# K and V of all four groups of the first batch made plainly, and another written order

## The chip, the cores and the metric

The kernel runs on one core of one Trainium2 chip. The metric is the device time of one execution in microseconds; the median of several executions is compared. The core has five engines with instruction streams of their own: TensorE (PE in the profile, with its weight loads as PEld), VectorE (DVE), ScalarE (ACT), GpSimd (POOL) and SyncE (SP), which here only issues transfers.

## The reference

A cross-attention block with four batches, 512 queries, 512 keys and a width of 512 (16 heads of 32), all in fp32:

```python
x = layer_norm(hidden, ln1_w, ln1_b)
q, k, v = x @ q_w + q_b, enc @ k_w + k_b, enc @ v_w + v_b      # split into 16 heads of 32
attn = softmax(where(mask, q @ k.T / sqrt(32), -max))
hidden = (attn @ v) @ cproj_w + cproj_b + hidden
y = layer_norm(hidden, ln2_w, ln2_b)
return hidden + gelu(y @ fc_w + fc_b) @ proj_w + proj_b        # inner width 2048
```

## The kernel before

The 16 heads are taken in four groups of four, and a batch's four groups give 16 steps called w (w = 4 x batch + group). For each w the kernel makes K, V and q (a product of the group's 128 weight columns with the transposed encoder or input tile), then four score steps, one per row tile of 128 queries. What is called "0:3" below is row tile 3 of w = 0. A score step is four products of 32 rows, one per head (L581). A softmax tile per head follows: DVE adds the mask and finds the minimum (L589), ACT takes the exponential (L592). The tiles are then transposed in blocks of 32 on DVE (L600, L607; L610 for the row sums), POOL copies the blocks that stay on their partitions (L617), twelve transfers of SP exchange the others, and PE multiplies with V (the attend, L639); DVE scales by the sums (L645). Behind the four groups come the output projection (L445), LN2 (statistics L343 and L344 on DVE, deviation L351 and L359 on POOL, normalisation L364 on DVE, turns L371 on PE), and two layers of the MLP (L694).

K and V come in two ways. Plainly, by `prep_k` (four products of 512 columns, L481, evicted by ACT at L484) and `prep_v` (sixteen products of 128 columns, L492, evicted at L498), one group at a time. Or for a pair p of groups (p = w // 2) by `kv`: a scheme of Strassen's kind with seven products of half-size blocks instead of eight (L524). It needs sums of the encoder tile's blocks (`e_sums`) and of the two groups' weight blocks (`kv_sums`), all on POOL (L332, L335), and joins of the results (`k_join`, `v_join`), three parts copied from PSUM and two additions on DVE, of 128x512 and of 128x256 (L332). In the first batch, groups 0 and 1 are made plainly and groups 2 and 3 as a pair; in the later batches all are pairs.

What stands when on each engine is written out by hand as one long string of tokens, `ORDER`. Each token is a name with its indices and names a generator; meeting it runs the generator to its next yield, which records the instructions of one step. Engines run their own instructions in the order in which they were recorded:

```python
    for token in ORDER.split():
        if token not in begun:
            name, *rest = token.split(":")
            begun[token] = takes[name](*map(int, rest))
        if begun[token] is not None:
            next(begun[token], None)
```

The tokens that matter here: `pk:w` and `pv:w` (plain K and V), `k:p`, `v:p` (pairs), `ks:p`, `vs:p`, `es:b` (sums), `kj:p`, `vj:p` (joins), `wk:w`, `wq:w`, `wv:w` (weight loads), `q:w`, `u:w:t` (score step), `x:w:t` (its softmax tiles, one head at a time), `r` (transposes), `d`, `e`, `a` (stay, exchange, attend), `s2:b`, `r2:b`, `n2:b`, `t2:b` (LN2), `lh:b` (the residual rows of x), `f:b:c` (MLP).

Buffers set waits too. The weights of step w lie in one of two buffers per kind, by w % 2, so a load for w = 2 has to wait until the product of w = 0 is done. Rows of x share a ring of six. PSUM has four banks for scores and a ring of four for everything else.

Of the kernel before, what the change touches and what calls it, by code (L numbers as in the profile page):

```python
# [20 lines left out]
P = 128  # L21
# [39 lines left out]
pk:0 s1:0 s1:0 s1:0 s1:0 r1:0 n1:0 wk:2 pk:0 n1:0 n1:0 n1:0 pv:0 pk:1 pk:1 t1:0:1 t1:0:1 t1:0:0 t1:0:3 t1:0:0 t1:0:2  # L61
  m:0 qb t1:0:2 pv:0 t1:0:3 q:0 q:0 k:1
u:0:0 x:0:0 x:0:0 x:0:0 x:0:0 wk:3 wv:1 lx:2 wq:1 lx:1 pv:1 wv:2 wq:2 lf:0:1 lx:1 wv:3 lc r:0:0 r:0:0
u:0:1 q:1 x:0:1 x:0:1 x:0:1 x:0:1 r:0:1 r:0:1 q:1
u:0:2 ks:1 vb:0 ks:1 r:0:1 v:1 vj:1 r:0:1 pv:1 x:0:2 x:0:2 x:0:2 es:0 m:0 vs:1 es:0 ks:1 es:0 k:1 es:0 vs:1 x:0:2 vs:1
  vs:1 ks:1 d:0:0 d:0:0
u:0:3 s1:1 x:0:3 kj:1 v:1 k:1 x:0:3 kj:1 r:0:2 v:1 k:1 vj:1 r:0:2 x:0:3 x:0:3 r:0:3 v:1
u:1:0 kj:1 vj:1 kj:1 k:1 r:0:3 r:0:3 vj:1 v:1 vj:1 lx:1 wq:3 q:3 s1:1 r:0:3 x:1:0 x:1:0 q:3 x:1:0 x:1:0
u:1:1 e:0:0 e:0:0 le:1 e:0:0 lx:1 s1:1 s1:1 r:1:0 wk:4 lh:0 x:1:1 x:1:1 x:1:1 kj:1 x:1:1 kj:1 r:1:1 r:1:0 d:0:1 q:2
  d:0:1 le:1 es:1 vb:0 le:1 lf:0:3 wk:5 le:1 r1:1 es:1 es:1 es:1  # L70
u:1:2 ts:1 ts:1 e:0:1 e:0:1 x:1:2 r:1:1 r:1:1 x:1:2 r:1:1 e:0:1 ks:2 ts:1 ks:2 ks:2 k:2 a:0:0 q:2 x:1:2 x:1:2 a:0:0
  d:1:0
u:1:3 kj:2 x:1:3 x:1:3 k:2 k:2 kj:2 vj:1 r:1:2 x:1:3 x:1:3 r:1:3 r:1:2
u:2:0 x:2:0 r:1:3 wv:4 lt:1 lt:1 lt:1 e:1:0 lb:1 lb:1 a:0:1 k:2 kj:2 v:2 x:2:0 a:0:1 d:1:0 ks:2 na:1 x:2:0 x:2:0
u:2:1 r:1:3 x:2:1 kj:2 e:1:0 e:1:0 na:1 k:2 a:1:0 wa:1 x:2:1 r:1:3 r:2:0 kj:2 x:2:1 x:2:1 wa:1 na:1 r:2:0
u:2:2 x:2:2 wa:1 wq:4 lt:1 na:1 r:2:1 r:2:1 a:1:0 wa:1 x:2:2 x:2:2 d:1:1 q:4 x:2:2 r:2:1 r:2:1 kj:2
u:2:3 x:2:3 vj:2 x:2:3 wq:5 e:1:1 e:1:1 e:1:1 wk:7 wk:6 wv:5 d:1:1 d:2:0 r:2:2 x:2:3 x:2:3 vs:2 ks:3 vs:2 vs:2 ks:3
  vb:1 e:2:0 e:2:0 q:5 e:2:0 wq:7 d:2:0 vs:2 r:2:3 q:4 r:2:3 r:2:2 a:1:1
u:3:0 x:3:0 v:2 v:2 vj:2 a:1:1 x:3:0 r:2:3 x:3:0 x:3:0
u:3:1 x:3:1 x:3:1 r:2:3 r:3:0 a:2:0 v:2 vj:2 x:3:1 x:3:1 a:2:0  # L80
u:3:2 k:3 r:3:0 r:3:1 x:3:2 x:3:2 vj:2 v:2 q:5 r:3:1 x:3:2 kj:3 x:3:2
u:3:3 r:3:1 vj:2 r:3:1 vj:2 x:3:3 d:2:1 vb:1 ks:3 d:2:1 lf:0:0 wq:6 e:2:1 lh:0 e:2:1 e:2:1 e:3:0 e:3:0 e:3:0 wv:6
  x:3:3 d:3:0 d:3:0 s1:2 r:3:2 x:3:3 x:3:3 r:3:2 q:6 a:2:1
u:4:0 m:1 r:3:3 a:2:1 r:3:3 r:3:3 q:7 k:3 x:4:0 x:4:0 q:6 r:3:3 x:4:0 x:4:0
u:4:1 lx:2 r:4:0 wv:7 lt:2 vs:3 ks:3 a:3:0 k:3 x:4:1 q:7 x:4:1 x:4:1 x:4:1
u:4:2 r:4:0 r:4:1 a:3:0 x:4:2 c:0:1 kj:3 k:3 x:4:2 x:4:2 r:4:1 x:4:2 kj:3
u:4:3 lt:2 d:3:1 d:3:1 cb:0 cb:0 r:4:1 vs:3 vs:3 vs:3 r:4:1 d:4:0 vb:2 s1:2 x:4:3 d:4:0 c:0:1 c:0:0 e:3:1 e:3:1 e:3:1
  r:4:2 x:4:3 kj:3 v:3 k:3 lx:2 lf:0:1 lf:0:0 lf:0:3 lh:0 lh:0 cb:0 cb:0 e:4:0 e:4:0 lx:2 e:4:0 lf:0:2 fs:0:0 c:0:0
  r:4:3 kj:3 s2:0 x:4:3 x:4:3 s1:2 a:3:1 vj:3 v:3 v:3 a:3:1 kj:3 r:4:2 r:4:3 vj:3
u:5:0 v:3 r:4:3 s2:0 s1:2 c:0:2 x:5:0 x:5:0 vj:3 r:4:3 vb:2 fs:0:0 r1:2 x:5:0 wv:8 x:5:0 vj:3 r:5:0  # L90
u:5:1 v:3 x:5:1 vj:3 x:5:1 r:5:0 c:0:2 x:5:1 x:5:1 r:5:1 c:0:3 c:0:3 d:4:1 d:4:1 wk:8 le:2 le:2 wk:9 e:4:1 le:2 le:2
  c:0:0 c:0:1 es:2
u:5:2 a:4:0 ts:2 ts:2 k:4 kj:4 r:5:1 x:5:2 s2:0 x:5:2 x:5:2 s2:0 x:5:2 r:5:1 r:5:1 a:4:0 ks:4 es:2 ks:4 es:2 ks:4 ks:4
  es:2 c:0:3 k:4 r2:0 c:0:2 e:4:1 k:4
u:5:3 kj:4 k:4 kj:4 e:4:1 r:5:2 e:5:0 e:5:0 e:5:0 r:5:2 x:5:3 x:5:3 kj:4 vj:3 x:5:3 a:4:1 x:5:3
u:6:0 n2:0 x:6:0 n2:0 k:4 kj:4 n2:0 n2:0 t2:0:3 t2:0:0 t2:0:3 t2:0:0 t2:0:1 t2:0:2 r:5:3 x:6:0 x:6:0 x:6:0 r:5:3
# [924 lines left out]
```

## Time and profile before

| | |
|---|---|
| median of 3 runs | 764.81 us (762.33 to 766.98) |
| profiled execution | 765.29 us |
| its span | 763.5 us, mean granted clock 0.998 |
| ACT, POOL busy | 411.4 us, 431.5 us |
| DMA | 162.19 MB, mean 212 GB/s |

Busy times are of one profiled execution, from its first instruction to its last. A matmul's end is modelled, so a busy PE can still be a waiting one. Every fp32 matmul has two records, so a count of x8 in the chain of waits stands for four products. Line numbers are those of the kernel before.

### The profile page before, as it was taken

What the parts mean: (1) busy time and instruction counts of PE and PEld (TensorE: products, weight loads), DVE (VectorE), ACT (ScalarE), POOL (GpSimd) and SP (SyncE); (2) the same over time, 40 slices, a digit from 0 to 9 for tenths busy, and PEclk for the clock granted to TensorE, in tenths of its full rate; (3) what the DMA queues carried; (4) which work ended last, traced back from release to release, by engine and by line L of the source; (5) the groups of instructions that cost most, each with busy time, mean ns of one, the idle gap of its engine ahead of it and who ended that gap; (6) DMA issues with size and microseconds to landing.
All of it is one profiled execution on the core that took longest, in us unless ns stands there. A gap on an engine that the chain in (4) does not pass through costs nothing.

```text
span 763.5 us, 14364 instructions
## 1 busy us (share of the span) xinstructions
PE 750.3 (98%) x4953; PEld 548.2 (72%) x4953; DVE 614.5 (80%) x1238; ACT 411.4 (54%) x981; POOL 431.5 (57%) x473
## 2 busy tenths in 40 slices
PE   9999999989999999999999999999999999999998
PEld 6565444646576656776565776767889999999997
DVE  3799999999889889987969787736688789888773
ACT  2567666455998776868867788732234321111111
POOL 1678866876978496889576566894201122131331
PEclk9999999999999999999999999999999999999999
DMA  6788979886777978695785778799535666688565
GB/s 227 236 242 225 236 201 252 232 230 184 242 200 194 281 204 247 196 281 154 214 245 171 218 256 261 215 254 353 167 131 165 214 209 123 213 184 257 140 123 121
DMA packets 72134, 162.19 MB, mean 212 GB/s; under 512 B 11960, under 2 KB 24656, under 8 KB 70400
## 3 DMA queue, kind: packets, MB, share of 16 engines
q1 hardware_dynamic: 56864, 131.44, 58.5%
q0 software_dynamic: 15056, 29.84, 16.0%
q8 instruction: 39, 0.64, 0.3%
q14 instruction: 31, 0.25, 0.1%
q10 hardware_dynamic: 144, 0.02, 0.0%
HBM read 73.95 MB, written 25.18 MB: 130 GB/s over the span
## 4 chain that ended last, share of the span: by engine, by line
PE 87%; DMA 4%; DVE 3%; ACT 3%; SPq 1%; issue 1%; POOL 0%; DVEq 0%; POOLq 0%; ACTq 0%
PE acc L694 36%; PE sc L694 12%; PE acc L524 9%; PE sc L581 8%; PE acc L445 7%; PE acc L639 6%; PE acc L573 5%; DMA ext<-encT_dram 2%; SPq L329 1%; ACT ptt L592 1%; PE acc L371 1%; DVE ptt L589 1%; PE acc L481 1%; PE acc L492 1%; DMA gd<-st 1%
## 5 line engine op out<-in xcount | busy, mean ns | idle before, releaser
L592 ACT ACTIVATE ptt<-ptt,mn 128x512 f32<-128x512 f32 x256 | 182.9, 716 | 52.8 <-DVE mn L589 52.2
L589 DVE CUSTOM_DVE_ANT_0 ptt<-sc,mix 128x512 f32<-128x512 f32 x256 | 165.4, 678 | 21.3 <-PE sc L581 18.6
L617 POOL COPY swap<-swap 32x1088 f32<-32x1088 f32 x128 | 140.2, 1095 | 36.1 <-DVE swap L610 29.6
L720 ACT COPY st<-acc 128x256 f32<-128x256 f32 x128 | 46.1, 367 | 96.3 <-PE acc L694 85.7
L720 ACT COPY xn<-acc 128x128 f32<-128x128 f32 x100 | 24.1, 267 | 133.0 <-PE acc L694 129.3
L600 DVE STREAM_TRANSPOSE swap<-ptt 128x1024 f32<-128x1024 f32 x64 | 79.0, 1235 | 5.2 <-ACT st L746 1.2
L581 PE MATMUL sc<-pbt 32*128 32x512 f32 x512 | 82.0, 647 | 0.0
L607 DVE STREAM_TRANSPOSE swap<-ptt 128x1024 f32<-128x1024 f32 x64 | 78.3, 1223 | 0.6 <-ACT ptt L592 0.6
L748 POOL DMA_DIRECT2D gd<-st x32 | 23.7, 743 | 86.5 <-ACT st L746 65.7
L694 PE MATMUL acc<-ys,ws 128*128 128x256 f32 x256 | 63.4, 383 | 0.5 <-ACT st L720 0.5
L639 PE MATMUL acc<-swap,mix 128*32 128x256 f32 x1024 | 61.9, 382 | 0.9 <-DMA ext<-x_t_dram 0.6
L573 PE MATMUL acc<-ext,ptt 128*128 128x512 f32 x128 | 58.8, 600 | 1.4 <-DVE mn L589 0.8
L445 PE MATMUL acc<-mix 128*128 128x512 f32 x128 | 58.3, 601 | 0.0
L694 PE MATMUL acc<-yT,pbt 128*128 128x256 f32 x240 | 58.1, 383 | 0.0
L694 PEld LDWEIGHTS acc<-ys,ws 128*128 128x128 f32 x256 | 47.4, 190 | 13.1 <-ACT st L720 4.7
L639 PEld LDWEIGHTS acc<-swap,mix 128*32 128x32 f32 x1024 | 30.4, 109 | 33.5 <-issue 9.7
L694 PEld LDWEIGHTS acc<-yT,pbt 128*128 128x128 f32 x240 | 44.5, 190 | 13.7 <-issue 5.1
L906 POOL DMA_DIRECT2D swap<-xn x18 | 22.4, 1434 | 52.8 <-DVE xn L332 18.7
L592 ACT ACTIVATION_READ_ACCUMULATOR ptt<-ptt,mn 128x1 f32 x256 | 48.3, 189 | 0.0
L906 POOL DMA_DIRECT2D yT<-xn x15 | 18.3, 1547 | 48.5 <-DVE yT L332 17.9
L573 PEld LDWEIGHTS acc<-ext,ptt 128*128 128x128 f32 x128 | 23.3, 190 | 30.9 <-issue 23.3
L445 PEld LDWEIGHTS acc<-mix 128*128 128x128 f32 x128 | 23.2, 190 | 31.0 <-issue 28.6
(163 smaller groups left out, 1601.9 us busy)
## 6 DMA issues: line engine op xcount, KB each, us to landing
swap<-swap SPq DMA_DIRECT2D x384, 136.0 KB, 3.3
gd<-st POOLq DMA_DIRECT2D x32, 512.0 KB, 3.9
swap<-gd SPq DMA_DIRECT2D x12, 1024.0 KB, 6.9
pbt<-fc_w_dram SPq DMA_DIRECT2D x40, 256.0 KB, 4.6
xn<-x_dram SPq DMA_DIRECT2D x32, 256.0 KB, 3.9
ext<-fc_w_dram SPq DMA_DIRECT2D x24, 256.0 KB, 3.7
swap<-xn POOLq DMA_DIRECT2D x18, 256.0 KB, 4.7
ptt<-k_w_dram SPq DMA_DIRECT2D x16, 256.0 KB, 5.2
```

The lines of the kernel that those rows point to most:

```text
L445: nc.tensor.matmul(acc, oT[:, g, ts(t, P)], wc[:, g, :], start=(g == 0), stop=(g == NG - 1))
L524: nc.tensor.matmul(out_, i, j, start=(k + t == 0 and not more), stop=(k == 1), skip_group_check=more or t > 0)
L573: nc.tensor.matmul(acc, S["wq", w][:, d, :], xT[:, d, :], start=(d == 0), stop=(d == ND - 1))
L581: nc.tensor.matmul(sc[h], S["qT", w][r, ts(qt, P)], S["kT", w][r, :], start=True, stop=True)
L589: nc.vector.tensor_tensor_reduce(out=s, in0=sc[h], in1=mb, scale=1.0, scalar=FMAX, op0=ALU.add, op1=ALU.min, accum_out=mn)
L592: nc.scalar.activation(s, s, AF.Exp, bias=mn, scale=-1.0, accum_out=S["sums", w][:, qt, h : h + 1])
L600: nc.vector.transpose(*two_heads[0])
L607: nc.vector.transpose(*two_heads[1])
L617: nc.gpsimd.tensor_copy(pT[ts(i, HD), i], tb[ts(i, HD), i])
L639: nc.tensor.matmul(av[ts(h, HD), : 2 * P].rearrange(shape, **kw), v[:, t, ts(h, HD)], p[t][h], start=(t == 0), stop=(t == NT - 1),)
L694: nc.tensor.matmul(o, x[:, k], w, start=(k == 0 and not more), stop=(k == n - 1), skip_group_check=more)
L720: nc.scalar.copy(g[:, i], S["qa", *key])
```

## The change

Only the string `ORDER` differs. The tokens of the pair p = 1 and of the first batch's encoder sums are gone, and plain ones stand in their place; the string as a whole (2569 tokens before, 2543 now) is written anew in another sequence, in all batches. The number of tokens of every kind that differs:

| tokens | before | now |
|---|---|---|
| `k:1`, `v:1` | 5, 5 | 0, 0 |
| `kj:1`, `vj:1` | 6, 6 | 0, 0 |
| `ks:1`, `vs:1`, `es:0` | 4, 4, 4 | 0, 0, 0 |
| `pk:2`, `pk:3`, `pv:2`, `pv:3` | 0 | 2 each |

```diff
-u:0:1 q:1 x:0:1 x:0:1 x:0:1 x:0:1 r:0:1 r:0:1 q:1
-u:0:2 ks:1 vb:0 ks:1 r:0:1 v:1 vj:1 r:0:1 pv:1 x:0:2 x:0:2 x:0:2 es:0 m:0 vs:1 es:0 ks:1 es:0 k:1 es:0 vs:1 x:0:2 vs:1
...
+u:0:1 x:0:1 x:0:1 x:0:1 x:0:1 r:0:1 q:1
+u:0:2 pk:2 pk:3 r:0:1 q:1 r:0:1 r:0:1 x:0:2 x:0:2 x:0:2 x:0:2
...
```

In the rows below, line numbers of the kernel now are two higher than those of the kernel before (L481 is L483 now, L492 is L494, L524 is L526, L573 is L575, L581 is L583, and L343, L344, L364, L589 are L345, L346, L366, L591). `sc` are the score banks, `acc` the ring of four, `ext` the encoder and input tiles, `ptt` weights and softmax tiles, `pbt` K and q.

**TensorE, from q of group 0 (the first row) on.** Before:

```order
L573 MATMUL acc_79<-ext,ptt 128x512 x4
L524 MATMUL acc_78<-ext,ptt 128x256 x2
L581 MATMUL sc_74<-pbt 128x512
L581 MATMUL sc_75<-pbt 128x512
L581 MATMUL sc_76<-pbt 128x512
L581 MATMUL sc_77<-pbt 128x512
L492 MATMUL acc_80<-ptt,ext 128x128 x16
```

Now:

```order
L575 MATMUL acc_78<-ext,ptt 128x512 x4
L494 MATMUL acc_80<-ptt,ext 128x128 x16
L583 MATMUL sc_74<-pbt 128x512
L583 MATMUL sc_75<-pbt 128x512
L583 MATMUL sc_76<-pbt 128x512
L583 MATMUL sc_77<-pbt 128x512
L494 MATMUL acc_81<-ptt,ext 128x128 x16
L483 MATMUL acc_79<-ext,ptt 128x512 x4
```

Ahead of the first score step the pair's first product (two of 256 columns) is replaced by the whole plain V of group 2, and behind it the plain K of group 2 has come to V of group 1.

**TensorE, the third and fourth score step (0:2 and 0:3) and the product ahead of each.** Before:

```order
L573 MATMUL acc_81<-ext,ptt 128x512 x4
L581 MATMUL sc_74<-pbt 128x512
L581 MATMUL sc_75<-pbt 128x512
L581 MATMUL sc_76<-pbt 128x512
L581 MATMUL sc_77<-pbt 128x512
L524 MATMUL acc_79<-ptt,ext 128x128 x4
L524 MATMUL acc_81<-ext,ptt 128x256 x4
L581 MATMUL sc_74<-pbt 128x512
```

Now:

```order
L575 MATMUL acc_78<-ext,ptt 128x512 x4
L583 MATMUL sc_74<-pbt 128x512
L583 MATMUL sc_75<-pbt 128x512
L583 MATMUL sc_76<-pbt 128x512
L583 MATMUL sc_77<-pbt 128x512
L483 MATMUL acc_81<-ext,ptt 128x512 x4
L583 MATMUL sc_74<-pbt 128x512
```

Between the two steps stood the first products of the V and K pair; now the plain K of group 3 stands there. The first row in both is q of group 1.

**DVE, between the last LN2 statistics of the first batch (BN_AGGR) and the first LN2 normalisation (TENSOR_SCALAR).** Before, the end of that piece; its twelve rows are preceded by six more that lead back to the BN_AGGR (one softmax tile, and the rows L607, L610, L645, L600):

```order
L607 STREAM_TRANSPOSE swap<-ptt 128x2x4x4x32
L589 ISA ptt,mn_3_0_1441<-sc_74,mix 128x512
L589 ISA mn_3_0_1441 128x1
L589 ISA ptt,mn_3_1_1444<-sc_75,mix 128x512
L589 ISA mn_3_1_1444 128x1
L332 TENSOR_TENSOR pbt<-acc_78,pbt 128x2x256
L332 TENSOR_TENSOR mix<-acc_79,mix 128x256
L589 ISA ptt,mn_3_2_1449<-sc_76,mix 128x512
L589 ISA mn_3_2_1449 128x1
L589 ISA ptt,mn_3_3_1468<-sc_77,mix 128x512
L589 ISA mn_3_3_1468 128x1
L364 TENSOR_SCALAR xn_85<-xn_85,mv_0_1200,rs_0_1406 128x512
```

Now, the whole piece:

```order
L345 BN_STATS st_0_3_1392<-xn_85 128x6
L346 BN_AGGR mv_0_1235<-st_0_3_1392 128x2
L612 STREAM_TRANSPOSE swap<-mix 128x2x4x32
L602 STREAM_TRANSPOSE swap<-ptt 128x2x4x4x32
L591 ISA ptt,mn_3_0_1408<-sc_74,mix 128x512
L591 ISA mn_3_0_1408 128x1
L591 ISA ptt,mn_3_1_1411<-sc_75,mix 128x512
L591 ISA mn_3_1_1411 128x1
L366 TENSOR_SCALAR xn_82<-xn_82,mv_0_1235,rs_0_1402 128x512
```

The statistics and the normalisation have come closer together: one small and one large transpose and two softmax tiles (an L591 pair each) are left between them. The normalisation also stands ahead of the last two softmax tiles of step 5:3, where it stood behind them.

On SP, the loads of V weights for groups 2 and 1 now come first behind the mask, and a load of `lh:0` stands ahead of the K weights of group 2.

More of the change, by code (lines that the diff above doesn't have):

```diff
@@ L68 @@
[L68 to L96, printed above, removed]
@@ new lines @@
+u:8:0 k:5 kj:5 f:0:4 a:6:1 j:0:4 g:0:2 g:0:4 r:7:2 x:8:0 x:8:0 x:8:0 r:7:3 x:8:0 a:6:1 r:7:3
+u:8:1 kj:5 lx:3 wv:10 e:7:0 wv:11 e:7:0 wq:10 e:7:0 v:5 x:8:1 e:7:1 e:7:1 e:7:1 lf:1:0 lf:0:6 lf:0:5 d:7:0 vs:5 cb:1
+  vs:5 vb:4 g:0:2 vs:5 vb:3 fs:0:3 fs:0:3 fs:0:3 d:7:1 fs:0:3 cb:1 d:7:1 cb:1 f:0:3 r:8:0 x:8:1 x:8:1 x:8:1 j:0:4
+  a:7:0
+u:8:2 g:0:4 r:8:0 r:8:1 a:7:0 s1:3 x:8:2 x:8:2 j:0:3 c:1:0 c:1:0 v:5 f:0:3 f:0:3 vj:5 j:0:3 r:8:1 x:8:2 x:8:2 r:8:1
+  s2:1 r:8:2
+u:8:3 f:0:3 j:0:3 r:8:1 vs:5 v:5 d:8:0 d:8:0 g:0:4 j:0:3 f:0:3 j:0:3 x:8:3 a:7:1 x:8:3 vj:5 x:8:3 x:8:3 r:8:2 r:8:3
+  j:0:3
@@ new lines @@
+u:12:1 j:1:2 d:11:0 vs:7 vs:7 vs:7 d:11:1 d:11:1 f:1:2 q:13 j:1:2 g:1:2 r:12:0 r:12:0 x:12:1 q:13 x:12:1 j:1:2 x:12:1
+  vj:7 v:7 x:12:1
+u:12:2 r:12:1 r:12:1 x:12:2 x:12:2 x:12:2 v:7 a:11:0 a:11:1 vj:7 x:12:2
+u:12:3 lf:2:4 g:1:2 v:7 vj:7 r:12:2 a:11:0 r:12:1 r:12:1 x:12:3 lf:1:5 e:12:0 vj:7 c:2:0 cb:2 g:1:2 fs:1:3 d:12:0
+  x:12:3 x:12:3 x:12:3 a:11:1 c:2:0 fs:1:3 fs:1:3 fs:1:3
+u:13:0 f:1:3 v:7 g:1:1 vj:7 g:1:1 r:12:3 r:12:3 j:1:3 r:12:2 x:13:0 f:1:3 f:1:3 c:2:2 j:1:3 r:12:3 vj:7 x:13:0 r:12:3
+  x:13:0 x:13:0
```

280 lines of the change are left out of this document (148 added, 132 removed).

## The prediction

> **What bounds the kernel now.** I read the page's busy shares first, then the busy times of four stretches, then what the vector engine waits for in the second of them, then the chain of waits.
>
> ```profile
> PE 750.3 (98%) x4953; PEld 548.2 (72%) x4953; DVE 614.5 (80%) x1238; ACT 411.4 (54%) x981; POOL 431.5 (57%) x473
> ```
>
> (The stretches are cut at the start of the first softmax tile, of the fourth step's first tile, and where TensorE resumes behind the first LN2; columns are PE, PEld, DVE, ACT, POOL busy, granted clock, DMA share, GB/s.)
>
> ```profile
> 24.30:37.80 13.50, 13.50 (x80) 8.54 (x80) 13.37 (x32) 9.71 (x26) 6.86 (x9) 1.00 0.74 218
> 37.80:173.10 135.30, 129.15 (x834) 71.48 (x833) 130.18 (x286) 83.63 (x223) 105.00 (x110) 1.00 0.85 229
> 173.10:500.00 326.90, 325.07 (x2043) 214.52 (x2044) 274.05 (x580) 254.38 (x556) 240.12 (x270) 0.99 0.77 223
> 500.00:763.50 263.50, 259.67 (x1897) 238.43 (x1895) 189.78 (x325) 58.42 (x171) 73.00 (x74) 1.00 0.68 189
> ```
>
> TensorE (PE) reads 98% busy, but its weight loads (PEld) fill only 71.48 of 135.30 us in the second stretch, against 238.43 of 263.50 at the end. VectorE (DVE) fills 130.18 of those 135.30. So from 37.8 to 173.1 us two engines could be the limit, and the waits say which:
>
> ```profile
> DVE pbt L332 <- ACT pbt L722: 1.0, 2, 0.8
> DVE ptt L589 <- PE sc L581: 0.8, 4, 0.3
> DVE swap L600 <- DMA ext<-x_t_dram: 0.8, 1, 0.8
> ```
>
> (waiter, released by: us in total, times, longest.) These are the three largest; DVE waits for nothing longer than 0.8 us and for TensorE 0.8 us in all. It is DVE that runs through here. The chain, in order of time (start, us, what), shows how it is entered and left:
>
> ```profile
> 9.89 3.57 PE acc L492 x32
> 13.46 3.44 PE acc L481 x8
> 18.90 3.44 PE acc L573 x8
> 22.34 0.86 PE acc L524 x4
> 23.21 1.07 PE sc L581 x8
> 24.28 3.77 PE acc L492 x32
> 29.12 3.63 PE acc L573 x8
> 36.63 1.43 PE sc L581 x8
> 53.76 0.60 DVE ptt L589
> 55.93 1.15 DVE swap L600
> 57.08 1.14 DVE swap L607
> 169.66 3.42 DVE xn L364 x3
> 178.12 1.86 PE acc L639 x32
> ```
>
> The entry: up to the fourth score step (group 0, row tile 3, at 36.63) every piece is TensorE. Then the chain goes over softmax pieces (L589) and transposes (L600, L607). The exit: the LN2 normalisation of the first batch (L364, three in 3.42 us) ends at 173.1, TensorE's turns (L371) wait for it, and behind them TensorE keeps going to the end. So the time is a sum of three: TensorE up to the fourth score step, DVE from there to the LN2 normalisation, TensorE from its turns to the end. The change moves all three.
>
> **Term 1, TensorE in front: +6.4 us.** After the same start (q of group 0 ends at 22.34 in both orders) the old order has two light products (0.86) ahead of the first scores, and its fourth score step starts 14.29 later. The new order puts the plain V of group 2 (sixteen 128-column products as in the L492 row, 3.57), a score step (1.07), V of group 1 (3.57), K of group 2 (four 512-column products, L481, 3.44), a score step, q of group 1 (L573, 3.44), a score step and K of group 3 (3.44) ahead of it: 3.57+1.07+3.57+3.44+1.07+3.44+1.07+3.44 = 20.67. That is 6.38 more. The old rows for V and q there read 3.77 and 3.63, 0.2 over their clean value; with that on all five big products it is 7.4, my upper end. Is DVE really late by all of it? Its first softmax tile moves by 3.57-0.86 = 2.7, from 24.3 to 27.0; up to the fourth step's scores it had 13.37 us of work in the old order (first row of the stretches) and has one transpose (1.15) more in the new one, so it is through at 41.5. The scores come at 22.34+20.67 = 43.0 and about 1.1 later reach DVE, as in the old order (36.63 to 37.8). So it stands for some 2.5 us, and TensorE sets the term. If the scores were ready sooner, DVE's own work would still make it 2.7+1.15 = 3.9, the lower end.
>
> The load of group 2's V weights can add to this. It reuses group 0's buffer, so the queue sends it only when V of group 0 is done, about 13.5; it must be there at 22.34.
>
> ```profile
> ptt<-v_w_dram SPq DMA_DIRECT2D x16, 256.0 KB, 4.2
> ```
>
> Such a load lands 4.2 us after its issue (median), so 4.6 us are to spare and I take nothing. The residual load of x that now goes ahead of the K weights of group 2 waits for the first turns (done at 18.90); those weights are wanted only at 30.6, eleven microseconds on.
>
> **Term 2, DVE: -7.1 us.**
>
> ```profile
> L332 DVE TENSOR_TENSOR pbt<-acc,pbt 128x512 f32<-128x512 f32 x7 | 4.8, 690 | 2.5 <-ACT pbt L722 2.5
> L332 DVE TENSOR_TENSOR mix<-acc,mix 128x512 f32<-128x512 f32 x7 | 4.8, 682 | 4.7 <-ACT mix L720 4.6
> L332 DVE TENSOR_TENSOR mix<-acc,mix 128x256 f32<-128x256 f32 x7 | 2.8, 407 | 3.5 <-PE acc L524 3.5
> L332 DVE TENSOR_TENSOR pbt<-acc,pbt 128x256 f32<-128x256 f32 x7 | 2.8, 404 | 0.0
> L343 DVE BATCH_NORM_STATS2 st<-xn 128x6 f32<-128x512 f32 x32 | 21.6, 674 | 9.0 <-DMA xn<-x_dram 9.0
> L344 DVE BATCH_NORM_AGGREGATE mv<-st 128x2 f32<-128x6 f32 x32 | 5.8, 182 | 1.1
> ```
>
> Removed: the joins of one K pair and one V pair, 0.690+0.404+0.682+0.407 = 2.18. Moved out of the stretch, counted from the two orders: one statistics pair to the front (0.674+0.182 = 0.86), one transpose to the front and one behind (1.15+1.14 = 2.29), and three softmax tiles (3 x 0.60 = 1.80) behind the LN2 normalisation, which now stands earlier among them. Sum 7.13. What was moved is not won: the front pieces lie in term 1, those behind are no longer on the path because TensorE is the fuller engine there. The uncertain part is the waits: the three rows above make 2.6 us. The new order could lose them all or have as much again, so the ends are -9.7 and -4.5.
>
> **Term 3, TensorE behind: +2.9 us.** From the LN2 turns on the new order has one more score step (1.07) and one more attend (L639, 1.86); all other products are the same in number. Their order is rewritten in all later batches too. TensorE was busy there for 325.07 of 326.90 and 259.67 of 263.50 us, so a better order has little to win; I take nothing for it.
>
> The TensorE work added is in terms 1 and 3 already. On its own it is small: two K products pairwise plain are 2 x 3.44 = 6.88 against fourteen 256-column products, and V 2 x 3.57 = 7.14 against twenty-eight 128-column ones at 3.57/16 = 0.223, which is 6.25.
>
> ```profile
> 218.73 2.59 PE acc L694 x12
> ```
>
> Six 256-column products take 2.59, so fourteen take 6.04, and the whole adds 0.84+0.89 = 1.73 us.
>
> **At nothing:** GpSimd (POOL) loses the four sums of the encoder tile and the eight of the weights.
>
> ```profile
> L332 POOL TENSOR_TENSOR ws<-ptt 128x256 f32<-128x256 f32 x14 | 10.4, 743 | 25.1 <-DMA ptt<-v_w_dram 15.6 <-DMA ptt<-k_w_dram 6.0 <-PE acc L524 3.3
> L335 POOL TENSOR_TENSOR mix<-ext,mix 128x512 f32<-128x512 f32 x8 | 10.3, 1286 | 5.5 <-DMA ext<-encT_dram 5.5
> ```
>
> About 8 x 0.74 + 4 x 1.28 = 11 us. It is busy 105.00 of 135.30 and none of DVE's three largest waits names it, so I take no gain; what hides it is DVE's own work. Were that cover gone, the gain would be what GpSimd holds DVE up, which is rival 1. ScalarE loses eight small evictions and gets four large ones; it is busy 83.63 of 135.30, and the one wait that names it (1.0) is in term 2's ends.
>
> **The sum:** 6.4 - 7.1 + 2.9 = +2.2 us on a profiled execution of 765.29 (span 763.5, the rest lies around it): 767.5. The median shown is 0.48 lower, so I forecast 767.0, no change by a bound of 0.5% (3.8 us), which is about what a measurement can tell. With one term at its end at a time the sum runs from 6.4-9.7+2.9 = -0.4 to 6.4-4.5+2.9 = +4.8, so 764.4 to 769.6 for this case alone.
>
> **A rule weighed against the trace.** The granted clock fell once:
>
> ```profile
> 172.00:174.00 2.00, 0.99 (x6) 0.56 (x6) 2.00 (x2) 0.50 (x1) 1.94 (x3) 1.00 0.01 2
> 174.00:176.00 2.00, 1.67 (x8) 1.39 (x8) 2.00 (x8) 2.00 (x5) 1.47 (x3) 0.62 0.00 0
> 176.00:178.00 2.00, 2.00 (x9) 0.52 (x8) 2.00 (x6) 1.37 (x5) 0.00 (x0) 0.52 0.60 182
> ```
>
> 0.62 and 0.52 in two stretches of 2 us, right behind TensorE's wait for LN2 (busy for 0.99 of 2.00): 2 x 0.38 + 2 x 0.48 = 1.7 us of clock lost. The Trainium skill, "TensorE: Matmul & The Clock Gate" (Part 1: The HAM clock gate), says that about 3.4 us of idleness halve the clock. By it an order that gives TensorE less to do between 40 and 173 us, as this one does, could be throttled once more, and the sum would be 768.7. In this trace the fall came behind about one microsecond of idleness: it bears out a fall behind idleness, but not that length. By the rows alone, one fall as before, the sum stays at 767.0, and I take that.
>
> **The rivals.**
>
> 1. Slower, by a wait at the LN2 normalisation. The rows of GpSimd and DVE there (start, us):
>
> ```profile
> 158.81 0.18 DVE L344 BATCH_NORM_AGGREGATE mv<-st 128x2 f32<-128x6 f32 x1
> 157.34 1.27 POOL L335 TENSOR_TENSOR mix<-ext,mix 128x512 f32<-128x512 f32 x1 [3.67 <-DMA ext<-encT_dram]
> 163.84 0.19 POOL L351 TENSOR_SCALAR ve<-mv 128x4 f32<-128x4 f32 x1
> 164.11 1.04 POOL L359 TENSOR_TENSOR rs<-ve,nhalf 128x4 f32<-128x4 f32 x1
> 168.15 0.91 DVE L364 TENSOR_SCALAR xn<-xn,mv,rs 128x512 f32<-128x512 f32 x1
> ```
>
> The last statistics end at 158.99. GpSimd, which stood 3.67 us for an encoder load, gives the deviation at 165.15, 6.16 later; DVE had other work until 168.15 and felt nothing. In the new order only a small transpose, a large one (1.15) and two softmax tiles (2 x 0.60) lie between; with the small one at a third of the large, 2.8. If GpSimd is as late again, DVE stands 3.4 us, with all softmax work queued behind it, and the time is 767.0+3.4 = 770.4. It decides from a wait of 1.6 us on. For it: the encoder loads still come late in the queue. Against it: GpSimd has 11 us less to do before that. Chance 0.29.
>
> 2. Faster. The normalisation rows ran at twice their usual length:
>
> ```profile
> L364 DVE TENSOR_SCALAR xn<-xn,mv,rs x20: 529/546/1314, 13.8 to 533.0; 128x512 f32<-128x512 f32 x20
> ```
>
> (min/median/max ns.) Three in 3.42 and one in 0.91 are 4.33 where four medians are 2.18. If nothing holds them up in the new place, 2.1 us go, and if the half clock goes with TensorE's shorter wait, 1.7 more: 763.2. The Trainium skill, "SBUF — State Buffer" (Who interferes with whom), has such an operation and GpSimd's exclude each other on a shared port pair; the trace agrees, with 1.14 us each for the three while GpSimd was busy, against a median of 0.546. Against this rival: GpSimd has work queued at the new place too. Chance 0.16; with a shorter first term it goes past 761.
>
> 3. A second fall of the clock: 767.0+1.7 = 768.7. For it the emptier TensorE, against it only one fall in the trace. Chance 0.08.
>
> 4. The change does not do what it says: were TensorE the limit throughout, the plain products would add their 1.73 and nothing else: 766.5. The waits of DVE speak against it. Chance 0.05.
>
> My own case keeps 0.42.
>
> **The numbers.** Slower by over 0.5% (above 768.6): most of rival 1 (0.26), half of rival 3 (0.05), the upper edge of my case (0.06): 0.37. Faster (below 761.0): the far half of rival 2, 0.09. Within: 0.54. The range goes from 762.0, a microsecond under rival 2, to 772.0, under two above rival 1.
>
> **What would show it.** Right: the first softmax tile starts 2.7 us later (3.57 less 0.86), the fourth score step at about 43; DVE shows idle time for TensorE of some 3 us before 45 and almost none from there to LN2; LN2's last normalisation ends at 173.1+6.4-7.1, about 172.4; TensorE does not wait behind it. Wrong: DVE idle for GpSimd's deviation (rival 1), clock rows under 0.9 at another place (rival 3), the normalisations at 0.55 (rival 2), or a TensorE that waits long behind 180, where I expect both orders to be equally full.

## The result, and the profile after

The new kernel took 775.57 us (median of 4 executions, 773.95 to 779.34) against 765.25 us for the one before (4): ratio 1.0143, 95% interval 1.0107 to 1.0179. Measured once more, beside other runs, it took 774.12 against 763.68: 1.0144 (1.0125 to 1.0163). It is slower by 10.3 and 10.4 us. My forecast was 767.0, and the range ended at 772.0.

The profiled execution took 779.34 us (span 777.5), the longest of all eight. I therefore read a second one beside it, of 773.69 us (span 771.9). First the page's busy shares, then the same four stretches as before, cut at the same events (columns: PE, PEld, DVE, ACT, POOL busy, granted clock, DMA share, GB/s):

```profile
PE 760.2 (98%) x4949; PEld 551.0 (71%) x4949; DVE 615.1 (79%) x1234; ACT 408.2 (52%) x975; POOL 423.2 (54%) x461
```

```profile
26.60:44.20 17.60, 17.60 (x81) 8.74 (x81) 14.46 (x33) 11.29 (x29) 5.10 (x5) 1.00 0.44 140
44.20:177.50 133.30, 125.75 (x764) 68.61 (x761) 123.70 (x272) 79.69 (x209) 96.97 (x103) 0.95 0.84 225
177.50:500.00 322.50, 317.73 (x1967) 206.19 (x1966) 266.38 (x566) 242.82 (x539) 233.38 (x258) 0.99 0.76 216
500.00:777.50 277.50, 274.15 (x2017) 249.75 (x2015) 201.58 (x346) 68.98 (x193) 83.71 (x87) 1.00 0.70 191
```

DVE now stands 9.6 us of the second stretch (133.30 less 123.70), where it stood 5.1, and the clock there is 0.95 instead of 1.00. The fourth score step on TensorE, and DVE at the first LN2:

```profile
39.46 3.70 PE L483 MATMUL acc<-ext,ptt 128*128 128x512 f32 x8
43.09 1.14 PE L583 MATMUL sc<-pbt 32*128 32x512 f32 x8
```

```profile
168.96 0.18 DVE L346 BATCH_NORM_AGGREGATE mv<-st 128x2 f32<-128x6 f32 x1
172.15 3.60 DVE L366 TENSOR_SCALAR xn<-xn,mv,rs 128x512 f32<-128x512 f32 x3 [0.27 <-POOL rs L361]
175.67 0.68 DVE L334 TENSOR_TENSOR pbt<-acc,pbt 128x512 f32<-128x512 f32 x1
176.27 1.23 DVE L366 TENSOR_SCALAR xn<-xn,mv,rs 128x512 f32<-128x512 f32 x1
```

The score step starts at 43.09, where 43.0 was forecast. LN2 ends at 177.5 instead of the forecast 172.4, although DVE waits only 0.27 us for the deviation. The granted clock, in stretches of 2 us of the same execution:

```profile
56.00:58.00 2.00, 2.00 (x22) 1.02 (x25) 2.00 (x5) 0.47 (x2) 1.82 (x2) 0.56 1.07 325
80.00:82.00 2.00, 2.00 (x24) 1.29 (x24) 2.00 (x3) 0.19 (x2) 1.07 (x1) 0.53 0.87 262
102.00:104.00 2.00, 2.00 (x10) 1.94 (x10) 2.00 (x7) 1.25 (x3) 0.84 (x1) 0.50 0.35 125
104.00:106.00 2.00, 2.00 (x11) 2.00 (x11) 2.00 (x3) 0.00 (x0) 1.88 (x3) 0.50 0.90 205
446.00:448.00 2.00, 0.00 (x0) 0.00 (x0) 0.07 (x1) 0.00 (x0) 1.92 (x3) 1.00 1.02 380
450.00:452.00 2.00, 2.00 (x8) 0.99 (x10) 0.88 (x2) 1.46 (x5) 0.23 (x1) 0.50 1.05 333
452.00:454.00 2.00, 2.00 (x10) 0.68 (x3) 1.11 (x4) 0.00 (x0) 0.00 (x0) 0.50 1.03 234
```

Four falls to half instead of one. Two lasted about 3.4 us, two about twice that; below, a window is 3.4 us at half clock, with 1.7 us of clock lost. Behind 180 us, what TensorE waits for from 200 to 500 us, in the second profiled execution of the new kernel and then in the kernel before:

```profile
PE acc L696 <- ACT st L722: 2.6, 1, 2.6
PE acc L696 <- POOL pbt L337: 1.2, 2, 0.9
PE acc L373 <- DVE xn L366: 0.9, 1, 0.9
```

```profile
PE acc L694 <- ACT st L720: 0.5, 1, 0.5
```

4.7 us of waits instead of 0.5, in the part for which I took nothing. (`L722` copies the results of the MLP out of PSUM into the tile from which a gelu result is stored; `L337` on GpSimd adds blocks of the MLP's weights.)

**How late TensorE is, at equal work left.** Steps stand at other places in the two orders, so their start times do not compare well. I summed the clean durations of the products still to come (0.858 us for 512 columns, others in proportion, 1.07 a score step, 1.86 an attend) and looked up when that sum passed a value. The table gives the time in the profiled execution of the kernel before, and how much later (+) each other kernel's profiled execution passed it. The letters are the experiments below; "again" is the second execution of the new kernel. Some records of products are missing from the traces, so the entries are good to some 0.7 us.

| work left, us | before, at | new | new again | e1 | e2 | g1 | h1 | h2 |
|---|---|---|---|---|---|---|---|---|
| 535 | 205.9 | +5.7 | +2.7 | +1.5 | -2.6 | -1.6 | -1.1 | -4.4 |
| 415 | 330.7 | +6.8 | +4.6 | +1.6 | -1.8 | -1.6 | +0.6 | -4.0 |
| 340 | 408.2 | +7.7 | +5.5 | +2.8 | -0.8 | +0.7 | +1.5 | -3.0 |
| 310 | 439.4 | +12.8 | +8.3 | +2.8 | +4.0 | +0.7 | +2.2 | +1.0 |
| 100 | 656.1 | +14.0 | +8.3 | +4.6 | +6.5 | +0.4 | +2.4 | +2.5 |

The ordinary execution ("new again") is 2.7 us late at 206 us, about the sum I forecast for the whole kernel (2.2). It then loses 2.8 up to 408 us and another 2.8 from there to 439. Single executions of one order differ too: g1, e1 and the kernel before have the same order behind 206 us, and g1 drifts there from -1.6 to +0.4, e1 from +1.5 to +4.6; e2, h1 and h2 have the order of the kernel before up to 190 us, and stand between -1.1 and -4.4 at 206.

### The profile page after: what moved, and what is told of

Read it like the earlier page. It is cut to its first block, busy times and chain, and to the rows that moved or that the text cites. A ratio compares the mean times of both kernels' runs of the same rounds, so it can differ in the third digit from the quotient of the medians.

```text
span 777.5 us, 14361 instructions
## 1 busy us (share of the span) xinstructions
PE 760.2 (98%) x4949; PEld 551.0 (71%) x4949; DVE 615.1 (79%) x1234; ACT 408.2 (52%) x975; POOL 423.2 (54%) x461
## 4 chain that ended last, share of the span: by engine, by line
PE 78%; issue 5%; DVE 5%; DMA 5%; ACT 4%; POOL 2%; SPq 1%; DVEq 0%; POOLq 0%; ACTq 0%
PE acc L696 31%; PE sc L696 11%; PE acc L526 8%; PE sc L583 7%; PE acc L447 6%; PE acc L641 6%; PE acc L575 5%; ACT ptt L594 2%; PE acc L494 1%; DMA swap<-swap 1%; DVE xn L366 1%; DMA ext<-encT_dram 1%; DVE ptt L591 1%; DMA pbt<-fc_w_dram 1%; SPq L331 1%
## 5 line engine op out<-in xcount | busy, mean ns | idle before, releaser
L591 DVE CUSTOM_DVE_ANT_0 ptt<-sc,mix 128x512 f32<-128x512 f32 x256 | 164.9, 677 | 31.5 <-PE sc L583 25.3
L722 ACT COPY st<-acc 128x256 f32<-128x256 f32 x128 | 46.1, 367 | 109.8 <-PE acc L696 74.8
L722 ACT COPY xn<-acc 128x128 f32<-128x128 f32 x100 | 24.3, 268 | 129.9 <-PE acc L696 128.1
L583 PE MATMUL sc<-pbt 32*128 32x512 f32 x512 | 84.2, 649 | 0.8 <-DVE mn L591 0.8
L641 PE MATMUL acc<-swap,mix 128*32 128x256 f32 x1024 | 64.7, 397 | 3.4 <-DMA swap<-swap 3.4
L575 PE MATMUL acc<-ext,ptt 128*128 128x512 f32 x128 | 59.1, 603 | 0.0
L583 PEld LDWEIGHTS sc<-pbt 32*128 32x128 f32 x512 | 25.1, 184 | 34.1 <-DVE mn L591 15.3
L575 PEld LDWEIGHTS acc<-ext,ptt 128*128 128x128 f32 x128 | 23.1, 189 | 32.0 <-issue 26.3
L748 ACT ACTIVATE st<-st,vec 128x512 f32<-128x512 f32 x64 | 44.1, 718 | 2.0 <-DVE st L334 1.4
```

Source lines behind the costliest of these rows:

```text
L575: nc.tensor.matmul(acc, S["wq", w][:, d, :], xT[:, d, :], start=(d == 0), stop=(d == ND - 1))
L583: nc.tensor.matmul(sc[h], S["qT", w][r, ts(qt, P)], S["kT", w][r, :], start=True, stop=True)
L591: nc.vector.tensor_tensor_reduce(out=s, in0=sc[h], in1=mb, scale=1.0, scalar=FMAX, op0=ALU.add, op1=ALU.min, accum_out=mn)
L641: nc.tensor.matmul(av[ts(h, HD), : 2 * P].rearrange(shape, **kw), v[:, t, ts(h, HD)], p[t][h], start=(t == 0), stop=(t == NT - 1),)
L722: nc.scalar.copy(g[:, i], S["qa", *key])
```

## The experiments

Each ran six to twelve times beside the kernel before (four or five times where so said); kernels that share a value under "before" ran on one chip. "Lost clock" is span x (1 - granted clock), the mean over a kernel's executions; over all runs the kernel before loses 0.9 us. Line numbers differ by up to three from those of the kernel before. The expectations, recorded ahead of each run, weigh three theories. A: the late part of the new order has waits of its own. B: all of the loss arises up to the LN2 of the first batch. C: falls of the granted clock make most of it.

| run | median, us | before, us | ratio (95%) | lost clock, us |
|---|---|---|---|---|
| e4 plain K, V in the old order | 773.22 | 763.73 | 1.0117 (1.0083, 1.0151) | 4.2 |
| g1 the same, one load later | 765.52 | 763.68 | 1.0027 (1.0003, 1.0050) | 0.6 |
| e3 new order, plain K, V later | 785.61 | 763.73 | 1.0273 (1.0242, 1.0304) | 10.1 |
| e1 new, then old from 6:2 | 772.62 | 763.73 | 1.0109 (1.0082, 1.0137) | 5.5 |
| e2 old, then new from 6:2 | 770.92 | 763.73 | 1.0093 (1.0066, 1.0119) | 3.1 |
| h1 new from 6:2 to 13:2 alone | 767.71 | 763.90 | 1.0049 (1.0030, 1.0069) | 1.3 |
| h2 new from 13:2 alone | 769.34 | 763.90 | 1.0069 (1.0043, 1.0095) | 0.4 |
| h3 new, then old from 13:2 | 771.54 | 763.90 | 1.0108 (1.0076, 1.0140) | 5.3 |
| f1 e2 with stores first | 770.51 | 762.72 | 1.0090 (1.0066, 1.0114) | 1.3 |
| f2 new with stores first (5) | 774.49 | 762.72 | 1.0156 (1.0128, 1.0183) | 6.0 |
| f3 new with filler (5) | 785.56 | 762.72 | 1.0296 (1.0271, 1.0321) | 3.3 |
| f4 before with filler | 776.69 | 762.72 | 1.0171 (1.0143, 1.0198) | 0.8 |
| g2 new with three repairs | 773.26 | 763.68 | 1.0125 (1.0105, 1.0146) | 3.6 |
| g3 e1 with two repairs | 771.43 | 763.68 | 1.0121 (1.0097, 1.0145) | 3.7 |
| g4 new, again (4) | 774.12 | 763.68 | 1.0144 (1.0125, 1.0163) | 4.8 |

**K and V alone: e4, g1 and e3.** In e4 the pair's tokens in the old order are replaced, and nothing else is moved:

```diff
-u:0:2 ks:1 vb:0 ks:1 r:0:1 v:1 vj:1 r:0:1 pv:1 x:0:2 x:0:2 x:0:2 es:0 m:0 vs:1 es:0 ks:1 es:0 k:1 es:0 vs:1 x:0:2 vs:1
+u:0:2 vb:0 r:0:1 r:0:1 pv:1 x:0:2 x:0:2 x:0:2 m:0 pk:2 x:0:2 d:0:0 d:0:0
...
+u:0:3 s1:1 x:0:3 pk:2 x:0:3 r:0:2 pv:2 pk:3 r:0:2 x:0:3 x:0:3 r:0:3 pv:2
+u:1:0 pk:3 r:0:3 r:0:3 pv:3 lx:1 wq:3 q:3 pv:3 s1:1 r:0:3 x:1:0 x:1:0 q:3 x:1:0 x:1:0
```

> The order of the kernel before with the pair of groups 2 and 3 replaced in place by the four plain products, one K ahead of the fourth score step and the others at the places of the pair's later products; no other token is moved. It prices K and V alone: two joins of each kind less on DVE (2.18 us), 1.73 us more on TensorE, 11 us less on GpSimd. If the plain products themselves cost time, 767 or more; if the rewriting of the rest is what costs (theories A and C), 763 to 765.5.

773.22, 9.5 us slower, far above the 767 at which I would have called the plain products dear. SP's queue in e4 (issues in order of time), the load of the encoder tile in the kernel before, and what DVE waits for in e4 from 40 to 60 us:

```profile
34.31 5.04 SPq L327 DMA_DIRECT2D swap<-swap  x8
49.73 0.35 SPq L327 DMA_DIRECT2D ext<-encT_dram  x1
50.12 2.41 SPq L327 DMA_DIRECT2D swap<-swap  x4
52.58 0.58 SPq L327 DMA_DIRECT2D xn<-x_dram  x1
```

```profile
39.89 0.34 SPq L329 DMA_DIRECT2D ext<-encT_dram  x1
```

```profile
DVE st L341 <- DMA xn<-x_dram: 5.5, 1, 5.5
```

SP stands from 39.4 to 49.7 at the load of the next encoder tile. That load overwrites the old tile, and the last plain V, which reads it, runs from 46.5 to about 50. In the kernel before, whose pair is done with the tile's blocks one after another, the first such load goes at 39.9. Behind the load stand four exchanges and the rows of x that DVE then lacks for 5.5 us. The Trainium skill, "DMA: Bandwidth & Descriptors" (Anatomy of one DMA), says, where it tells of the path through GpSimd, that a transfer's wait is held by the issuing sequencer before dispatch; SP's queue agrees, with 10.3 us. In g1 that one token moves:

```diff
-u:1:1 e:0:0 e:0:0 le:1 e:0:0 lx:1 s1:1 s1:1 r:1:0 wk:4 lh:0 x:1:1
+u:1:1 e:0:0 e:0:0 e:0:0 lx:1 s1:1 s1:1 r:1:0 wk:4 lh:0 le:1 x:1:1
```

> Run e4 (old order, plain K and V) with one entry of SP's queue moved: the first load of the next batch's encoder tile, which has to wait until the plain V of group 3 has read the old one, stands behind the last exchange of group 0, the rows of x and two weight loads instead of ahead of them. In e4 SP stands 10.3 us at it (39.4 to 49.7), and VectorE 5.5 us for the rows of x behind it; the lag to the kernel before grows from 2 to 6 us there. If the blocked queue is the price of plain K and V: the lag stays near 2 us, LN2 of the first batch at about 172 instead of 176.5, and 773.2 becomes 767 to 769. If it is TensorE's own work: 772 to 774.

```profile
33.98 7.57 SPq L327 DMA_DIRECT2D swap<-swap  x12
41.60 0.59 SPq L327 DMA_DIRECT2D xn<-x_dram  x1
49.40 1.28 SPq L327 DMA_DIRECT2D ext<-encT_dram  x3
```

The exchanges and the rows are out before the same load waits, and 765.52 remains: 1.8 us over the kernel before, better than the 767 to 769 that I expected. The blocked queue was worth 7.7 of the 9.5 us, by way of the clock too, of which e4 loses 4.2 us and g1 0.6. What is left (0.2 to 3.8 us by the interval) agrees with the 1.73 us that I had counted as extra TensorE work; the 2.18 us of joins that DVE lost and GpSimd's 11 us bought nothing that shows. e3 moves the four plain products of the new order behind the fourth score step:

```diff
-lh:0 wk:2 wq:1 pv:2
+lh:0 wk:2 wq:1
...
-u:0:2 pk:2 pk:3 r:0:1 q:1
+u:0:2 r:0:1 q:1
...
-u:0:3 pv:2 pv:3 r:0:2 x:0:3 x:0:3 pk:3 x:0:3 x:0:3 s1:1 pv:3
-u:1:0 r:0:3 d:0:0
+u:0:3 pv:2 r:0:2 x:0:3 x:0:3 x:0:3 x:0:3 s1:1 pv:2 pk:2
+u:1:0 pk:2 pv:3 r:0:3 d:0:0
...
-e:0:0 q:3 e:0:0 e:0:0 le:1
+e:0:0 q:3 e:0:0 e:0:0 pv:3 pk:3 pk:3 le:1
```

> The new order with only the plain V and K products of groups 2 and 3 moved: all four stand behind the fourth score step instead of three of them (V of 2, K of 2, K of 3) ahead of it. My term 1 (+6.4) should go: the fourth score step at about 33 to 34 instead of 43. Theory B: that is won at the LN2 of the first batch too (about 171 instead of 177.5), and the time is 769 to 770. Rival: DVE meets the same work later and waits there for K and V, so that LN2 ends at 175 or later and the time stays at 773 to 776. Theory A has the late loss of 6 to 7 us unchanged in both cases.

My term 1 is gone there (the softmax of 0:3 starts at 38.4, before at 37.8), and yet the time is 785.61. SP stands 15.1 us for the plain K of group 3, and the first softmax tile of step 1:3 starts 13 us later than in the kernel before. Making the products early, which I had counted as a price, is what keeps the queue open. In the new kernel it is open: from 40 to 80 us SP's longest wait is 1.8 us. So a queue that is blocked there is not what makes the new kernel slow.

**Which part of the rewriting costs: e1, e2, h1, h2, h3.** These join the two orders at score steps 6:2 (about 190 us) and 13:2 (about 405). Tokens that would be lost or stand twice at a joint are set in or left out at it or behind it, up to eight of each. As an example, e1 from its joint on:

```diff
-u:6:2 r:6:1 r:6:0 lb:2 lb:2 lx:3 wk:11 wv:9 lt:2
+u:6:2 lh:1 lt:2 wv:9 lb:2 wq:8 lb:2 e:5:1 e:5:1
...
```

> The new order up to the score step 6:2 (in the middle of the second batch), and from there the order of the kernel before, so the early part is the new one and the late part the old one. Theory A (the late part of the new order has waits of its own, about 6.7 us of the loss): 768 to 770 us against 765 for the kernel before, the LN2 normalisation of the first batch ending at about 177.5 as in the new order, and the last 587 us as in the old. Theory B (all of the loss arises up to the LN2 of the first batch, or follows from its disturbed beginning): 773 to 776. Theory C (falls of TensorE's granted clock make most of the loss, wherever TensorE is emptied): the time follows the number of half-clock stretches, 3 to 4 us of the loss left if those at 443 to 451 go.

> The reverse: the order of the kernel before up to the score step 6:2, with K and V of groups 2 and 3 as a pair, and from there the new order. Theory A: 771 to 772 us, LN2 of the first batch at about 173 as before, GpSimd standing some 15 us for one store near 405 to 420 and TensorE waiting some 3 us near 440 to 450. Theory B: 765 to 766, since nothing early is touched. Theory C: 771 or more if the clock falls again behind the late wait, 768 if it does not.

Both alone are slow, by 8.9 and 7.2 us, and the whole by 10.4, so neither theory held alone and the parts do not add up. e1's six executions had one to five windows of half clock. The one with a single window, which was profiled, has LN2 as I forecast (172.4):

```profile
166.57 3.60 DVE L364 TENSOR_SCALAR xn<-xn,mv,rs 128x512 f32<-128x512 f32 x3 [0.23 <-POOL rs L359]
170.69 1.22 DVE L364 TENSOR_SCALAR xn<-xn,mv,rs 128x512 f32<-128x512 f32 x1
```

It ends at 171.9. With the same instructions up to there it was 174.5 (new again), 175.4 (f2) and 176.7 (h3) in executions with three windows, and 177.5 in the one with four. The later part was then halved:

> The old order up to 6:2, the new one up to 13:2 (about 190 to 405 us), and the old one behind. If the loss of e2 (7.2 us) is spread over the later batches: 766 to 768 against 764. If it sits behind 13:2: 763 to 765. By the traces TensorE lags by 2 to 3 us more at 424 us than at 206 in the new order, so I expect 766.

> The old order up to 13:2 and the new one behind (about 405 to 530 us). The waits seen there in the traces: 1.7 to 3.2 us at 436 to 446 for a gelu store, with a half clock behind it in some executions, and about 1.1 at 483. If they are the loss: 768 to 770. If the loss needs the new middle ahead of it: 764 to 766.

> The new order up to 13:2 and the old one behind. If the last piece costs 4 us by itself: 770 instead of 774. If the old last piece meets work that is already late: 773 to 775.

The loss is in both halves: 3.8 us for the middle alone, 5.4 for the last piece, and h3 gets 2.6 of the new kernel's 774.1 back. h1 and h2 lose hardly more clock than the kernel before, or less, so lost clock is not what makes these two slow. What TensorE waits for in h2, from 200 to 500 us:

```profile
PE acc L691 <- ACT st L717: 2.1, 2, 1.5
PE acc L691 <- POOL pbt L332: 1.9, 2, 1.1
PE acc L691 <- DMA pbt<-fc_w_dram: 0.5, 1, 0.5
```

A joint may have a price of its own: behind 206 us e1 follows the old order and still loses 3.1 us, though g1, without a joint, loses 2.0 of that too (table above). So the pieces are upper ends.

**The late wait and the clock: f1 and f2.** In e2, TensorE waits 3.2 us for ScalarE, which waits for a store of a gelu result to free its buffer, and the clock falls in it, at 439 us, to half for 6.8 us (waits of both from 425 to 460 us; one stretch of 2 us):

```profile
ACT st L718 <- DMA gd<-st: 5.1, 1, 5.1
```

```profile
PE acc L692 <- ACT st L718: 3.2, 1, 3.2
```

```profile
442.00:444.00 2.00, 2.00 (x10) 0.52 (x8) 1.31 (x2) 0.65 (x3) 0.00 (x0) 0.50 1.05 275
```

f1 and f2 issue both stores ahead of GpSimd's other work:

```diff
-r2:2 g:1:5 g:1:4 d:13:1 g:1:5 d:13:1
+g:1:5 g:1:4 g:1:5 r2:2 d:13:1 d:13:1
```

> The kernel of run e2 (old order up to 6:2, then the new one), with one swap on GpSimd near 433 us: the two stores of the gelu results stand ahead of LN2's deviation of the third batch and of two stay copies, instead of one of them behind. In e2 ScalarE waits 5.1 us for such a store, and with it TensorE 3.2 us, and the clock then stands at half for 6.8 us. The store should come 3 to 4 us sooner, so TensorE's wait goes. Theory C (the wait pulls the clock down): 3.2 us of wait and 3.4 us of lost clock go, 771 becomes 764 to 765. If the clock is not tied to that wait: 767 to 768. If the late loss sits elsewhere (GpSimd's stand of 15 us near 400): still 770 to 771.

> The same swap in the new order as a whole. The late loss is the same wait there (3.4 us and 6.8 us of half clock), so by theory C 775.6 becomes 769 to 770, by the wait alone 772, and no change if it sits elsewhere.

In f1's profile TensorE waits 1.7 us instead of 3.2, and the clock stays up:

```profile
PE acc L692 <- ACT st L718: 1.7, 1, 1.7
```

```profile
444.00:446.00 2.00, 2.00 (x13) 0.82 (x12) 0.83 (x3) 1.69 (x6) 1.84 (x3) 1.00 1.01 370
```

Every execution of e2 lost 3.1 us of clock, f1's lost 1.3 on the mean. The median moved from 770.92 to 770.51 (ratio 1.0093 to 1.0090), and f2 not measurably. So in e2 the fall goes with the wait, and yet my price for it (3 to 6 us) was wrong: for the new kernel it was not typical, since "new again" has no fall near 440 us. Where f1's gain went I can't say; its profiled LN2 ended 4.5 us later than e2's with the same instructions ahead, so two single profiles don't settle it.

The last branch of f1's expectation is the one that came true: that the loss sits at a stand of GpSimd near 400 us. GpSimd issues the gelu stores. In every kernel with both new late pieces it stands 15.1 us for one of them, until ScalarE is ready ("new again"; then the longest wait of GpSimd from 340 to 480 us in the kernel before):

```profile
POOL gd L750 <- ACT mix L607: 15.1, 1, 15.1
```

```profile
POOL xn L332 <- DMA xn<-x_dram: 6.5, 1, 6.5
```

In h2 the stand is 10.2 us. From 420 us on GpSimd works without a wait ("new again"), and it issues the store for which ScalarE and TensorE then stand at 440.2, 1.9 us after ScalarE wrote the last result. f1 shows that this is not the whole: its stores go 0.6 us after the results, and TensorE still waits 1.7 us, until the store has landed. What the stand costs by the weight sums behind it, for which TensorE waits 1.2 us in both, no run tested.

**Is TensorE empty between 45 and 130 us? f3 and f4.** Useless work, the q products of w = 2 to 5 done twice:

```diff
-        for d in range(ND):
+        for d in [*range(ND)] * (2 if w in (2, 3, 4, 5) else 1):
             nc.tensor.matmul(acc, S["wq", w][:, d, :], xT[:, d, :], start=(d == 0), stop=(d == ND - 1))
```

> The new order with useless TensorE work: the q products of w = 2 to 5 are done twice (the second pass overwrites the first), 4 x 3.44 = 13.8 us more for TensorE between about 50 and 130 us, where it waits for VectorE. Theory C: TensorE is no longer empty there, the half-clock stretches before 110 us go (four of them in the profiled run), LN2 of the first batch ends at about 172 to 174 instead of 177.5, and the time falls to 770 to 773 although there is more work. Theory B (the structure of the order loses the time, the clock only shows it): TensorE's slack is used up in places, 776 to 785.

> The control: the same doubled q products in the kernel before, whose clock falls once or not at all. It prices what the useless work itself costs: 764 to 767 if TensorE's slack in that stretch swallows it, up to 777 if it does not. What f3 shows is to be read against this.

The control decides: in the old order the 13.8 us of useless work cost 14.0. From 40 to 130 us, the kernel before and then f4 (columns as above), and DVE's longest wait in f4 there:

```profile
40.00:130.00 90.00, 87.08 (x554) 46.64 (x552) 86.75 (x195) 59.93 (x159) 66.58 (x66) 1.00 0.86 230
```

```profile
40.00:130.00 90.00, 87.66 (x512) 45.85 (x511) 74.69 (x166) 49.85 (x131) 57.14 (x57) 1.00 0.72 192
```

```profile
DVE ptt L588 <- PE sc L580: 13.3, 6, 3.7
```

DVE, full before, now waits 13.3 us for scores. TensorE had no room at those places: a q product stands directly ahead of a score step, and DVE has nothing else to do until the scores come. f3 loses 3.3 us of clock instead of 6.0 (both sets of the new kernel), and its filler costs some 11 us instead of 14, so the higher clock may have paid back some of it.

**Two attends moved: g2 and g3.**

```diff
-u:2:1 a:0:1 r:1:3 na:1 r:1:3 x:2:1 na:1 a:1:0 x:2:1 r:2:0
-u:2:2 r:2:0 q:4
+u:2:1 a:0:1 r:1:3 na:1 r:1:3 x:2:1 na:1 x:2:1 r:2:0
+u:2:2 r:2:0 a:1:0 q:4
...
-r:2:3 x:2:3 r:2:2 a:1:1
-u:3:0 x:3:0
+r:2:3 x:2:3 r:2:2
+u:3:0 a:1:1 x:3:0
```

> The new order with the swap of f2 and two moves on TensorE in the first batch: the attend of group 1, at which TensorE stands 2.7 to 3.9 us near 77 us for the exchange, goes behind the next score step, and the next attend goes between the score steps 3:0 and 3:1, where TensorE stands 1.3 us for a free bank. Theory C: with these waits the half-clock stretches at about 78 and 100 us go too (three of 3.4 us), and 775 becomes 768 to 770. If the waits matter without the clock: 771 to 773. Rival: VectorE is the limit there, the waits go elsewhere: 774 to 776.

> Run e1 (new order to 6:2, then the old one) with the same two moves of attends. In e1 the clock fell between one and five times in an execution, and its time went with that, from 770.2 to 774.6. Theory C: zero or one fall in nearly all executions, 768 to 769.5 with less spread. Rival (chance falls that no order here prevents): 772 to 773 with the same spread.

> The new kernel once more, unchanged, for a second profiled execution and five more times beside the other three on one chip. Theory C: a clock lower by 0.006 to 0.014 than that of the kernel before, in stretches behind the waits near 77, 96 and 440 us, and 774 to 777. If the profiled execution of 779.3 was a stray one, the late stretch of 6.8 us is absent here.

The rivals were right: no gain that can be told from nothing (1.0144 to 1.0125 for g2, 1.0109 to 1.0121 for g3), with fewer windows of half clock, but not without. In g3 the wait for the exchange is gone, and others stand in its place (TensorE, 60 to 100 us):

```profile
PE acc L524 <- DVE pbt L332: 2.7, 1, 2.7
PE acc L524 <- POOL ws L335: 1.7, 1, 1.7
```

g4 is the "new again" of the tables: two to three windows of half clock in each execution, all of them early in the profiled one. No run here beats the kernel before.

## Why the prediction was wrong

**Term 1, TensorE in front: right.** 43.09 against 43.0, the first softmax tile at 26.6 against 27.0. DVE stood 3.1 us there (17.60 less 14.46), where some 3 were forecast. But the term was no mere loss: e3 shows that the early products are what lets SP's queue go on.

**Term 2, DVE: its size came out only where the clock hardly fell.** With one window of half clock LN2 ends at 171.9 (e1; forecast 172.4); in the four others named above, with three and four windows, at 174.5 to 177.5. The waits were not bounded by "as much again": in the first profile of the new kernel DVE stands 1.3 to 1.6 us each for the exchange, GpSimd, ScalarE and TensorE. And DVE's saving is worth less than I counted: g1 takes 2.18 us of joins away and gains nothing that shows, and f4 fits that: TensorE had no room either. My reading that DVE alone "runs through" from 38 to 173 us was wrong; TensorE's weight loads filling half the time do not mean that TensorE has room.

**Term 3, "so a better order has little to win; I take nothing for it": this step failed.** It looked at what a better order could win, when the order could as well be worse. In the ordinary execution of the new kernel it cost 5.6 us (lag 2.7 to 8.3). TensorE waits there 4.7 us, for a gelu store, for weight sums and for LN2, where it waited 0.5 in the kernel before. The 5.6 come from one pair of executions, and g1 drifts by 2.0 with the old order there; but the medians of h1 and h2, 3.8 and 5.4 us over the kernel before, show the middle and the last piece each to be slower alone, without lost clock. A TensorE that waits behind 180 us was the last on my list of what would show the forecast wrong. Which token of the late part starts these waits is not shown.

**Extra TensorE work, 1.73 us: right in size as far as g1 tells, and on the path.** g1 measures 1.8 (0.2 to 3.8). For K and V alone, rival 4 (TensorE the limit throughout) gives g1's time.

**GpSimd at nothing: right.** Rival 1 had the place right, 3.0 us from the statistics to the normalisation where it had 2.8, but not the lateness of GpSimd: 0.27 us of waiting. Rival 2 did not happen: the normalisations still took 3.60 us for three.

**The clock: rival 3 was priced as one more fall, with 0.08** (half of which is 0.04, not the 0.05 of the chances' sum). The new kernel loses 6.0 us of clock (eight executions) against 0.9. Over 102 executions of the new kernel and the experiments, each taken against its own set's mean, a lost microsecond goes with 0.74 us of time (standard error 0.12). By that the clock is some 4 of the 10.4 us. This is a correlation; no run held the clock up and left all else alone. The rest is not split further: the parts priced alone (e1, h1, h2) come to 18.1 us, more than the whole.

## What to carry to other kernels

When a buffer is held longer, look up the load that refills it and read what stands behind that load in its queue: in e4 one token's place there was worth 7.7 us, four times the price of the work. An order rewritten where an engine is 98% busy can hardly gain and can lose, as this one did, so such a rewriting should get a price range that lies on one side of nothing. And whether a busy engine has room is learned by giving it useless work at the place in question, not from its weight loads or its shares.

## What the runs showed of the hardware that was not expected

The half clock comes in windows of about 3.4 us, alone or two together, and the same wait may bring it or not (the wait for the gelu store: one window at 2.0 us in g2, none at 2.6 in "new again"). Two kernels with the same instructions up to 190 us, f2 and then e1, at TensorE's wait for the exchange near 77 us and in the stretch behind it:

```profile
77.03 2.97 PE L639 MATMUL acc<-swap,mix 128*32 128x256 f32 x32 [2.19 <-DMA swap<-swap]
```

```profile
78.00:80.00 2.00, 2.00 (x21) 0.88 (x13) 2.00 (x7) 0.52 (x1) 1.92 (x2) 0.50 0.85 226
```

```profile
77.19 1.93 PE L639 MATMUL acc<-swap,mix 128*32 128x256 f32 x32 [2.21 <-DMA swap<-swap]
```

```profile
78.00:80.00 2.00, 2.00 (x27) 1.34 (x17) 2.00 (x5) 0.36 (x1) 1.66 (x2) 1.00 0.89 227
```

2.2 us of waiting in both; the clock is 0.50 in one and 1.00 in the other. The Trainium skill, "TensorE: Matmul & The Clock Gate" (Part 1: The HAM clock gate), gives a window of about 3.4 us for both, an idle one that halves the clock and a busy one that restores it. The length of the falls agrees with that, but here they came behind shorter waits too, such as the 2.19 us in f2. Executions of one order also part where a load lands: with the same instructions ahead, three normalisations of LN2 took 2.03 us in e2, and 3.49 in f1, whose GpSimd had stood 3.60 us for an encoder load (0.21 in e2) and was at a sum and two copies beside them:

```profile
168.51 2.03 DVE L362 TENSOR_SCALAR xn<-xn,mv,rs 128x512 f32<-128x512 f32 x3
```

```profile
159.29 1.28 POOL L333 TENSOR_TENSOR mix<-ext,mix 128x512 f32<-128x512 f32 x1 [3.60 <-DMA ext<-encT_dram]
```

```profile
171.56 3.49 DVE L362 TENSOR_SCALAR xn<-xn,mv,rs 128x512 f32<-128x512 f32 x3
```
